# A transformer encoder-decoder layer: the two score pieces of a pair side by side, other shares of copies between VectorE and ScalarE

## The chip, the cores and the metric

The kernel runs on one core of a Trainium2 chip. TensorE multiplies matrices and transposes, VectorE and ScalarE read its results from PSUM (eight banks of 512 float32 for each of 128 partitions), GpSimd works on SBUF only, and SyncE (SP) issues the DMAs. The metric is the device time in microseconds of one execution; the figure of a kernel is the median of its runs.

## The reference

All is float32. A context of 2 x 77 rows goes through one encoder layer; 2 x 2048 rows of 512 features go through one decoder layer that attends to itself (causal) and to the context. There are 16 heads of 32.

```python
def _mha(xq, xkv, w_in, b_in, w_out, b_out, bias):
    q, k, v = ...                                   # projections, split into H heads
    scores = jnp.einsum('bhqd,bhkd->bhqk', q, k) / jnp.sqrt(hd)
    attn = jax.nn.softmax(scores + bias[None], axis=-1)
    return jnp.einsum('bhqk,bhkd->bhqd', attn, v)... @ w_out.T + b_out

x = ctx;  x = x + mha(ln(x), ln(x), bias=eb);  memory = x + ff(ln(x))
y = y + mha(ln(y), ln(y), bias=sb + causal)         # 2048 x 2048
y = y + mha(ln(y), memory, bias=cb)                 # 2048 x 77
y = y + relu(ln(y) @ ff1.T + b1) @ ff2.T + b2       # 512 -> 2048 -> 512
```

The position bias depends on the distance of query and key alone and is constant from a distance of 127 on.

## The kernel before, in words

The order of the instructions is written out by hand in Python loops; each engine works off its own queue in that order, and semaphores hold it where data or space is missing.

**Part one: causal self-attention** (to about 1,777 us), with the small encoder threaded in between. The rows of each of two batches are cut into four blocks `m` of 512 queries. For each block, each group `g` of four heads and each query tile `t` of 128 there is a *unit* (`units`). A unit in which the query tile has index `i = 4 m + t` sees `i + 1` key tiles. `pieces(i)` cuts these into pieces of at most four key tiles (512 columns); so units have one piece in a first block, two in a second, three in a third, and three or four in a fourth. Three steps work on pieces:

- `scores` (L344): four matmuls (L361), one for each head of the group, into four PSUM banks; each has 32 rows of contraction, so the four run in different row groups of the array. VectorE then evicts each bank: L370 copies the columns that need no bias into `pp` and takes the maximum with it; in the last piece of a unit, L377 does it for the 256 nearest columns with the bias added, and L384 makes the maximum of the row. For a last piece, four exps (L387, ScalarE, in place in `pp`) follow; in later blocks they are not issued at once but kept in `late_exps`, from which `exps(k)` takes k.
- `turn` (L397): the transposes of the probabilities (L411), four to a bank, and the copy of each bank to `pts` on VectorE (L415) or ScalarE (L417). A full pair of pieces has eight banks of them.
- `values` (L422): attention times V (L428), 16 matmuls for a piece of four key tiles, into a bank of its own (bank 7).

The other banks, 0 to 6, are handed out in turn by `bank()`; every step that needs a bank takes the next one, and waits until the last reader of that bank has done with it. `pp` holds the probabilities of two units, so unit `n` may be scored as far as unit `n - 2` has been turned (`may_score`, L1244).

The loop at L1262 takes the pieces of a unit in pairs. It scores what is missing, turns the pair, runs `slot(n + 1)` at the end of a unit (one projection job, L206, L217, L230 or L242, and light work such as norms, encoder stages, or the first block's cross-attention), scores one piece of a later unit, issues one or two kept exps, runs the values of the pair, and then scores further pieces if the pair had two.

**Part two: cross-attention and feed-forward of the eight blocks.** The feed-forward is done in quarter products with seven instead of eight multiplications (`PARTS`): `first_product` (L1128) has matmuls L1134, whose result is written to or accumulated in `hT` (L1145, L1147, L1149, L1151) and goes through the relu (L1154); `second_product` (L1156) has L1165 and L1173. `prepare` (L1106) forms sums of quarters (L1117) on GpSimd and VectorE three slots ahead. `ff_bank` takes banks 4 to 7 in turn. One product is done per slot; beside it, `cross(x)` (L1196) runs the next block's cross-attention by a plan of slots: norms (`norm_stages`, L718: statistics, centring L735, transposes L741, scaling and shift L745 and L747 per 128 columns), queries (`q_group`, L751), and for each of four query tiles `attend_stages` (L757): scores L768, bias and maximum L775 to L778, exp L781, division by the sum L786 to L788, transposes L794, values L805, output L814. The bias of a tile's place (`bias_tile`, L103, four DMAs) is loaded for the first two tiles of a batch's first block alone. The first block's cross-attention (`first_cross`) uses the same stages within part one.

Of the kernel before, what the change touches and what calls it, by code (L numbers as in the profile page):

```python
# [11 lines left out]
AF = mybir.ActivationFunctionType  # L12
# [5 lines left out]
P = 128  # L18
# [36 lines left out]
def tile_encoder_decoder(ctx: ExitStack, tc: tile.TileContext, ins, out):  # L55
# [93 lines left out]
    with (  # L149
# [247 lines left out]
        def turn(pieces):  # L397

            first = units[pieces[0][0]][1] == 0
            loads = []  # L400
            for n, k0, kn in pieces:
                ks = range(k0, k0 + kn)
                if first:
                    loads += [[(n, k, r) for k in ks] for r in range(HC)]
                else:
                    loads += [[(n, k, r) for r in range(HC)] for k in ks]
            for o, load in enumerate(loads):
                pt = bank()
                pts = in_turn("pts", pts_all).rearrange("p (x q) -> p x q", q=P)
                for x, (n, k, r) in enumerate(load):  # L410
                    nc.tensor.transpose(pt[:, ts(x, P)], state[n]["p"][r][:, ts(k, P)], ident)  # L411
                    got[n, k, r] = pts[:, x, :]
                w = len(load) * P
                if o % 2 if first else o >= (len(loads) + 1) // 2:
                    nc.vector.tensor_copy(pts[:, : len(load), :], pt[:, :w])  # L415
                else:
                    nc.scalar.copy(pts[:, : len(load), :], pt[:, :w])  # L417
                if o == min(3, len(loads) - 1):
                    exps(1)
            exps(1)  # L420

# [296 lines left out]
        def norm_stages(y, n, row, place, done):  # L718

            keep = {}  # L720

            def stats():
                st = sm.tile([P, 6], F32, name="bnst", tag="bnst")
                mv = sm.tile([P, 2], F32, name="cmv", tag="cmv", bufs=4)
                rs = sm.tile([P, 2], F32, name="crs", tag="crs", bufs=4)
                nc.vector.bn_stats(st, y())
                nc.vector.bn_aggr(mv, st)
                nc.vector.tensor_scalar_add(rs[:, 0:1], mv[:, 1:2], EPS)
                nc.gpsimd.tensor_tensor(rs[:, 1:2], rs[:, 0:1], mhalf[:, 0:1], ALU.pow)
                keep.update(mv=mv, rs=rs)  # L730

            def center():
                xn = keep["xn"] = place()
                mv, rs = keep["mv"], keep["rs"]
                nc.vector.tensor_scalar(xn, y(), mv[:, 0:1], rs[:, 1:2], ALU.subtract, ALU.mult)  # L735
                nc.gpsimd.tensor_tensor(y(), y(), row, ALU.add)

            def turned():
                xn, pt, dst = keep["xn"], bank(), done()
                for c in range(NC):  # L740
                    nc.tensor.transpose(pt[:, ts(c, P)], xn[:, ts(c, P)], ident)  # L741
                for c in range(NC):
                    sc, bi = vec(f"dec_{n}_s", c), vec(f"dec_{n}_b", c)
                    if c % 2:
                        nc.scalar.activation(dst[:, c, :], pt[:, ts(c, P)], AF.Identity, bias=bi, scale=sc)  # L745
                    else:
                        nc.vector.tensor_scalar(dst[:, c, :], pt[:, ts(c, P)], sc, bi, ALU.mult, ALU.add)  # L747

            return stats, center, turned

# [3 lines left out]
                nc.tensor.matmul(mm, w[:, c, :], nT[:, c, :], start=(c == 0), stop=(c == NC - 1))  # L754
            nc.vector.tensor_scalar(dst, mm, vec("dec_ca_in_b", o), SCALE, ALU.add, ALU.mult)

        def attend_stages(q, kTc, v, y, biased, pr, pts, place, w_o):  # L757

            prh = pr.rearrange("p (h k) -> p h k", k=S)
            by_r = pr.rearrange("p (g r k) -> p g r k", r=HC, k=S)  # L760
# [22 lines left out]
            def normalize():  # L783
                su = sm.tile([P, H], F32, name="csu", tag="csu", bufs=2)
                ri = sm.tile([P, H], F32, name="cri", tag="cri", bufs=2)
                nc.vector.tensor_reduce(su, prh, AX.X, ALU.add)  # L786
                nc.vector.reciprocal(ri, su)
                nc.gpsimd.tensor_tensor(prh, prh, ri[:, :, None].to_broadcast([P, H, S]), ALU.mult)  # L788

            def turned():  # L790
                for g in range(NC):
# [336 lines left out]
        def first_product(s):  # L1128
            x, layer, i, n = slots[s]
            a, b = operands[s]  # L1130
            mm = ff_bank()
            for f in range(2):
                for c in range(2):
                    nc.tensor.matmul(  # L1134
                        mm[:, ts(f, TOK)], a[:, c, ts(f, P)], b[:, c, :], start=(c == 0), stop=(c == 1)
                    )
            order = order_of(x, 1)
            got = mm.rearrange("p (f n) -> p f n", f=2)
            for k, (sign, r, c) in enumerate(PARTS[i][2]):
                users = [j for j in order if (r, c) in [u[1:] for u in PARTS[j][2]]]  # L1140
                f = (r - 1) * (NF // 2) + 2 * n
                dst = hT[:, f : f + 2, ts(c - 1, TOK)]
                if i == users[0]:
                    if sign == "-":
                        nc.scalar.activation(dst, got, AF.Identity, scale=-1.0)  # L1145
                    elif k:
                        nc.vector.tensor_copy(dst, got)  # L1147
                    else:
                        nc.scalar.copy(dst, got)  # L1149
                else:  # L1150
                    nc.vector.tensor_tensor(dst, dst, got, SIGN[sign])  # L1151
                if i == users[-1]:
                    for e in range(2):
                        nc.scalar.activation(dst[:, e, :], dst[:, e, :], AF.Relu, bias=vec("dec_ff1_b", f + e))  # L1154
# [41 lines left out]
        def cross(x):  # L1196
# [9 lines left out]
            def bias(t):  # L1206
                bias_tile(pr.rearrange("p (h k) -> p h k", k=S), 2, P, S, 255 - P * t)
# [9 lines left out]
            for t in range(TB):  # L1217
                at = 14 + 7 * t
                y = lambda t=t: y_of(x, t)
                biased = m == 0 and t < 2  # L1220
                if biased:
                    plan[at if t else at - 4].append(lambda t=t: bias(t))
                fs = attend_stages(
                    lambda g, t=t: qT[g // 2][:, g % 2, ts(t, P)], kTcs[b], vcs[b], y, biased, pr,
                    lambda g: pts_all[:S, g, :], place("xr"), wbt,
                )
                for k, f in zip((0, 2, 3, 6, 9, 11), fs):
                    plan[at + k].append(f)
                fs = norm_stages(y, "n3", bo, place("xt"), lambda t=t: nTt[:, :, ts(t, P)])
                for k, f in zip((13, 15, 17), fs):  # L1230
                    plan[at + k].append(f)
# [30 lines left out]
        while i < len(stream):  # L1262
# [17 lines left out]
            if may_score():  # L1280
                score_next()
            exps(2 if units[n][1] == 1 else 1)
            for p in pair:
                values(*p)
            while may_score() and (len(pair) > 1 or units[n][1] == 0):
                score_next()
            i += len(pair)

        xt_ring += [sb.tile([P, D], F32, name="xt", tag="xt", bufs=2) for _ in range(2)]
# [71 lines left out]
```

## Time and profile before

| | us |
|---|---|
| median of three runs (2929.42 to 2933.62) | 2931.29 |
| the profiled execution | 2935.85 |
| its span, first to last instruction | 2934.1 |
| PE busy (98%) | 2868.7 |
| DVE busy (75%) | 2205.3 |
| ACT busy (42%) | 1219.5 |
| POOL busy (25%) | 736.9 |
| mean granted TensorE clock | 0.991 |

PE is TensorE's matmuls, PEld its weight loads, DVE VectorE, ACT ScalarE, POOL GpSimd. Ends of matmuls are modelled, so a busy PE is not one at its peak; the pace is better read from the starts of one group of matmuls and the next. In a timeline line stand the start, the length, the engine, the line of the code and what is written from what, with the idle time ahead and what ended it in brackets.

### The profile page before, as it was taken

How to read it: one execution, taken by the hardware profiler on the slowest of the kernel's cores; microseconds unless marked ns; L12 is line 12 of the kernel's file. 1: busy time of each engine (PE TensorE's matmuls, PEld its weight loads, DVE VectorE, ACT ScalarE, POOL GpSimd, SP SyncE). 2: the span in 40 equal slices, each digit the busy share in tenths (PEclk: the TensorE clock that was granted, in tenths of full speed). 3: DMA queues.
4: the chain of work that ended last, by engine and by line, in shares of the span. 5: the costliest groups of instructions: out<-in, count | busy, mean ns of one | idle time of the engine just before them, and what ended most of it. 6: DMA issues, size and time to landing. Idle time of an engine off the chain costs nothing.

```text
span 2934.1 us, 60690 instructions
## 1 busy us (share of the span) xinstructions
PE 2868.7 (98%) x24440; PEld 2012.8 (69%) x24440; DVE 2205.3 (75%) x6171; ACT 1219.5 (42%) x2211; POOL 736.9 (25%) x601
## 2 busy tenths in 40 slices
PE   8899999999999999999999999999999899999999
PEld 5457666666666556666666667777777777777788
DVE  4767688878987788888888895767676767676765
ACT  3344456546665445565556672313131313131311
POOL 0100000000000101000000004555555464646465
PEclk9899999999999999999999999999999999999999
DMA  6413301201112502211101115000001000000000
GB/s 174 99 54 112 100 16 56 63 16 44 34 41 64 135 19 76 70 30 56 48 16 37 41 46 191 1 29 1 29 1 38 10 29 1 29 1 29 1 15 15
DMA packets 117644, 137.10 MB, mean 47 GB/s; under 512 B 18241, under 2 KB 73073, under 8 KB 117235
## 3 DMA queue, kind: packets, MB, share of 16 engines
q1 hardware_dynamic: 117362, 133.22, 15.7%
q8 instruction: 192, 3.15, 0.4%
q14 instruction: 90, 0.73, 0.1%
HBM read 111.33 MB, written 21.86 MB: 45 GB/s over the span
## 4 chain that ended last, share of the span: by engine, by line
PE 80%; DVE 13%; issue 2%; POOL 2%; ACT 2%; DMA 1%; SPq 0%; POOLq 0%; DVEq 0%; ACTq 0%
PE psum L1165 13%; PE psum L411 12%; PE psum L361 10%; PE psum L1134 8%; PE psum L428 7%; DVE pp L370 5%; PE psum L230 4%; PE psum L814 4%; PE psum L754 4%; PE psum L206 4%; PE psum L242 4%; PE psum L217 3%; DVE pp L377 3%; PE psum L794 2%; PE psum L805 1%
## 5 line engine op out<-in xcount | busy, mean ns | idle before, releaser
L387 ACT ACTIVATE pp<-pp,nm 128x128 f32<-128x128 f32 (+15 forms) x512 | 614.1, 1209 | 195.1 <-DVE nm L384 192.3
L370 DVE TENSOR_SCALAR_CACHE_REDUCE pp<-psum 128x512 f32<-128x512 f32 (+3 forms) x1024 | 558.0, 589 | 53.3 <-PE psum L361 51.5
L411 PE MATMUL psum<-ident,pp 128*128 128x128 f32 x4352 | 549.0, 279 | 18.0 <-DVE mx L377 11.8
L411 PEld LDWEIGHTS psum<-ident,pp 128*128 128x128 f32 x4352 | 474.5, 142 | 132.4 <-DVE pp L370 57.1
L417 ACT COPY pts<-psum 128x512 f32<-128x512 f32 (+3 forms) x592 | 298.7, 577 | 510.5 <-PE psum L411 401.3
L1117 POOL TENSOR_TENSOR vv<-pp 128x512 f32<-128x512 f32 x320 | 414.5, 1311 | 145.3 <-PE psum L1134 125.7
L361 PE MATMUL psum<-kT,q 32*128 32x512 f32 (+3 forms) x2560 | 353.5, 579 | 8.7 <-DVE mx L377 3.9
L415 DVE COPY pts<-psum 128x512 f32<-128x512 f32 (+2 forms) x544 | 329.9, 660 | 42.5 <-PE psum L411 40.8
L428 PEld LDWEIGHTS psum<-pts,vv 128*32 128x32 f32 x8704 | 226.2, 110 | 123.9 <-issue 116.9
L428 PE MATMUL psum<-pts,vv 128*32 128x128 f32 x8704 | 278.9, 276 | 0.0
L276 POOL TENSOR_TENSOR rstd<-rstd,mhalf 128x1 f32<-128x1 f32 x32 | 18.2, 570 | 919.9 <-DVE rstd L275 854.7
L1154 ACT ACTIVATE kT<-kT,vecs 128x256 f32<-128x256 f32 x256 | 115.2, 499 | 300.8 <-DVE kT L1151 300.8
L377 DVE CUSTOM_DVE_ANT_0 pp<-psum,bias 128x256 f32<-128x256 f32 (+1 forms) x512 | 209.6, 409 | 24.5 <-PE psum L361 16.6
L1151 DVE TENSOR_TENSOR kT<-kT,psum 128x512 f32<-128x512 f32 x256 | 166.4, 680 | 80.9 <-PE psum L1134 80.5
L361 PEld LDWEIGHTS psum<-kT,q 32*128 32x128 f32 x2560 | 119.6, 184 | 153.0 <-issue 99.3
L1165 PE MATMUL psum<-vv 128*128 128x256 f32 x768 | 176.9, 381 | 0.0
L1134 PE MATMUL psum<-oT,vv 128*128 128x256 f32 x736 | 166.5, 380 | 0.0
L1165 PEld LDWEIGHTS psum<-vv 128*128 128x128 f32 x768 | 143.1, 190 | 26.8 <-issue 9.5
L1134 PEld LDWEIGHTS psum<-oT,vv 128*128 128x128 f32 x736 | 138.8, 190 | 24.4 <-issue 6.2
L1117 DVE TENSOR_TENSOR vv<-kT 128x512 f32<-128x512 f32 x160 | 140.0, 892 | 10.8 <-PE psum L1165 9.8
L257 POOL TENSOR_TENSOR xr<-xr,row_dec_sa_out_b 128x512 f32<-128x512 f32 x30 | 38.1, 1274 | 375.1 <-DVE pts L415 244.3
L206 PE MATMUL psum<-nT,wqk 128*128 128x512 f32 x256 | 119.1, 609 | 0.0
(178 smaller groups left out, 3920.0 us busy)
## 6 DMA issues: line engine op xcount, KB each, us to landing
wqk<-in_dec_sa_in_wT_dram SPq DMA_DIRECT2D x64, 256.0 KB, 3.8
bias<-tz SPq DMA_DIRECT2D x128, 128.0 KB, 3.5
wbig<-in_dec_sa_in_wT_dram SPq DMA_DIRECT2D x8, 1024.0 KB, 7.3
vv<-in_enc_ff_wT_dram SPq DMA_DIRECT2D x8, 1024.0 KB, 5.4
wbig<-in_dec_sa_out_wT_dram SPq DMA_DIRECT2D x8, 1024.0 KB, 7.5
vv<-y SPq DMA_DIRECT2D x32, 256.0 KB, 3.5
out_dram<-vv SPq DMA_DIRECT2D x32, 256.0 KB, 2.0
xt<-in_x_dram SPq DMA_DIRECT2D x30, 256.0 KB, 3.9
```

Source lines behind the costliest of these rows:

```text
L206: nc.tensor.matmul(mm, w[:, c, :], nTs[b, m][:, c, :], start=(c == 0), stop=(c == NC - 1))
L361: nc.tensor.matmul(banks[r][:, : kn * P], q[rows4(r), ts(t, P)], kT[rows4(r), g, k0 * P : (k0 + kn) * P], start=True, stop=True,)
L370: nc.vector.tensor_scalar(p[:, k0 * P : (k0 + far) * P], s[:, : far * P], 1.0, None, ALU.mult, ALU.max, accum_out=st["mx"][:, r, c : c + 1],)
L377: nc.vector.tensor_tensor_reduce(p[:, (i + 1) * P - w : (i + 1) * P], s[:, far * P : kn * P], biases[b, m, g][:, r, 2 * P - w :], 1.0, LOW ...
L387: nc.scalar.activation(p, p, AF.Exp, bias=nm, accum_out=to)
L411: nc.tensor.transpose(pt[:, ts(x, P)], state[n]["p"][r][:, ts(k, P)], ident)
L415: nc.vector.tensor_copy(pts[:, : len(load), :], pt[:, :w])
L417: nc.scalar.copy(pts[:, : len(load), :], pt[:, :w])
L428: nc.tensor.matmul(ot[rows4(r), t, :], vv[:, k, ts(g * HC + r, HD)], got.pop((n, k, r)), start=(k == 0), stop=(k == i),)
L1117: engine.tensor_tensor(dst, quarter(*parts[0], n), quarter(*parts[2], n), SIGN[parts[1]])
L1134: nc.tensor.matmul(mm[:, ts(f, TOK)], a[:, c, ts(f, P)], b[:, c, :], start=(c == 0), stop=(c == 1))
L1165: nc.tensor.matmul(mm[:, t, :], lhs[:, c, ts(t, P)], rhs[:, c, :], start=(n == 0 and c == 0), stop=(n == 3 and c == 1),)
```

## The change

In part one: of the banks that a pair's turn copies, VectorE takes the first three of eight (`3 * len(loads) // 8`, rounded down; the last half before), ScalarE the others; no exp is issued amid the copies any more in later blocks; and the further pieces that may be scored are scored before the values of the pair instead of behind them, with one exp then.

In part two: all four scalings of a norm's transposes go to ScalarE (two of four were on VectorE; `first_cross` uses them too); the second of two first copies in `first_product` goes to ScalarE as well; the division of the first query tile of a block goes from GpSimd to VectorE; and the second tile's bias is loaded one slot earlier.

```diff
@@ turn
-                if o % 2 if first else o >= (len(loads) + 1) // 2:
+                if o % 2 if first else o < 3 * len(loads) // 8:
                     nc.vector.tensor_copy(pts[:, : len(load), :], pt[:, :w])
                 else:
                     nc.scalar.copy(pts[:, : len(load), :], pt[:, :w])
-                if o == min(3, len(loads) - 1):
+                if first and o == len(loads) - 1:
                     exps(1)
             exps(1)
@@ norm_stages, turned
-                    if c % 2:
-                        nc.scalar.activation(dst[:, c, :], pt[:, ts(c, P)], AF.Identity, bias=bi, scale=sc)
-                    else:
-                        nc.vector.tensor_scalar(dst[:, c, :], pt[:, ts(c, P)], sc, bi, ALU.mult, ALU.add)
+                    nc.scalar.activation(dst[:, c, :], pt[:, ts(c, P)], AF.Identity, bias=bi, scale=sc)
@@ attend_stages
-        def attend_stages(q, kTc, v, y, biased, pr, pts, place, w_o):
+        def attend_stages(q, kTc, v, y, biased, pr, pts, place, w_o, engine=None):
...
-                nc.gpsimd.tensor_tensor(prh, prh, ri[:, :, None].to_broadcast([P, H, S]), ALU.mult)
+                (engine or nc.gpsimd).tensor_tensor(prh, prh, ri[:, :, None].to_broadcast([P, H, S]), ALU.mult)
@@ first_product
-            for k, (sign, r, c) in enumerate(PARTS[i][2]):
+            for sign, r, c in PARTS[i][2]:
...
                     if sign == "-":
                         nc.scalar.activation(dst, got, AF.Identity, scale=-1.0)
-                    elif k:
-                        nc.vector.tensor_copy(dst, got)
                     else:
                         nc.scalar.copy(dst, got)
@@ cross
-                    plan[at if t else at - 4].append(lambda t=t: bias(t))
+                    plan[at - 1 if t else at - 4].append(lambda t=t: bias(t))
                 fs = attend_stages(
                     lambda g, t=t: qT[g // 2][:, g % 2, ts(t, P)], kTcs[b], vcs[b], y, biased, pr,
                     lambda g: pts_all[:S, g, :], place("xr"), wbt,
+                    None if t else nc.vector,
                 )
@@ the loop over pairs
             if may_score():
                 score_next()
             exps(2 if units[n][1] == 1 else 1)
+            while may_score() and (len(pair) > 1 or units[n][1] == 0):
+                score_next()
+            exps(1)
             for p in pair:
                 values(*p)
-            while may_score() and (len(pair) > 1 or units[n][1] == 0):
-                score_next()
             i += len(pair)
```

## The prediction

> **What bounds the kernel now.** I read the page's busy table first, then a table of stretches, then the timeline, group start against group start.
>
> ```profile
> PE 2868.7 (98%) x24440; PEld 2012.8 (69%) x24440; DVE 2205.3 (75%) x6171; ACT 1219.5 (42%) x2211; POOL 736.9 (25%) x601
> 650.00:860.00 210.00, 208.04 (x2393) 139.89 (x2393) 185.76 (x603) 128.75 (x177) 7.15 (x8) 0.98 0.12 35
> 2320.00:2934.00 614.00, 603.12 (x3497) 481.47 (x3496) 413.82 (x697) 132.25 (x259) 344.72 (x267) 1.00 0.04 15
> ```
>
> The columns of a stretch: its length, then busy PE, PEld, DVE, ACT, POOL, granted clock, DMA share, GB/s. TensorE is the bound in both parts; VectorE is at 88% in the attention of a fourth block and 67% in part two. So what counts is TensorE's stalls. Its unhindered pace is read from starts:
>
> ```profile
> 572.75 1.14 PE L361 MATMUL psum<-kT,q 32*128 32x512 f32 x8
> 573.82 1.96 PE L428 MATMUL psum<-pts,vv 128*32 128x128 f32 x64
> 575.70 1.14 PE L361 MATMUL psum<-kT,q 32*128 32x512 f32 x8
> 576.77 1.97 PE L411 MATMUL psum<-ident,pp 128*128 128x128 f32 x16
> ```
>
> Two score pieces (L361) with the values (L428) between: 1.07, 1.88, 1.07 us, no stall. Pieces of 384 and 256 columns take 0.86 and 0.645 so. A 512-column matmul has a pitch of 0.455 us (eight of L206 from 564.03 to 567.67); four heads run side by side, two matmuls each, so 0.91 of the 1.07 is work and 0.16 the step to the next kind of matmul.
>
> **Side by side: what it costs.** A piece takes four banks of a ring of seven. Two pieces with nothing between need eight: the second's fourth head writes the bank of the first's first head, and must wait until VectorE has evicted it (L370). Today the values stand in that gap. The order of the two programs' instructions gives 114 places with adjacent pieces after the change, 16 before. Those few show the price:
>
> ```profile
> 648.20 1.58 PE L361 MATMUL psum<-kT,q 32*128 32x512 f32 x14
> 649.36 0.69 DVE L370 TENSOR_SCALAR_CACHE_REDUCE pp<-psum 128x512 f32<-128x512 f32 x1 [0.32 <-PE psum L361]
> 650.11 0.29 PEld L361 LDWEIGHTS psum<-kT,q 32*128 32x128 f32 x2 [0.73 <-DVE pp L370]
> 1289.76 0.31 PEld L361 LDWEIGHTS psum<-kT,q 32*128 32x128 f32 x8 [0.20 <-issue]
> 1291.93 0.29 PEld L361 LDWEIGHTS psum<-kT,q 32*128 32x128 f32 x2 [0.50 <-DVE pp L370]
> 1292.98 0.20 PEld L411 LDWEIGHTS psum<-ident,pp 128*128 128x128 f32 x2 [0.76 <-DVE pp L370]
> ```
>
> At 648.20 VectorE was free: it starts 1.16 us after the piece (when the first scores are there) and the fourth head resumes at 1.91. With 0.91 of its own and 0.16 behind, 512 + 512 takes 2.98 us; at 1289.76, with VectorE in arrears, 3.22. Apart they take 2.14: +0.84 to +1.08. I take 0.93, nearer to the first: VectorE's three copies now come first and are done when the scores are. The other pairs likewise: 512 + 256 measured 2.70 against 1.72, unhindered 2.56: 0.9; 512 + 384 in between, 0.92; 384 + 256 measured 2.19 against 1.50: 0.69. New places: 48 x 0.93 + 22 x 0.92 + 12 x 0.9 + 10 x 0.69 = 44.6 + 20.2 + 10.8 + 6.9 = 82.5 us.
>
> With three pieces adjacent, the third waits for all four evictions of the first and one of the second. 384, 512, 512 (8 places; the first is a query tile's last piece, whose evictions take 0.74 each, below): banks free at 1.6, 2.34, 3.08, 3.82 and, one eviction (0.61, with 0.14 to the restart: 649.36, 649.97, 650.11) later, 4.65; with 0.91 + 0.16, 5.7 us against 0.86 + 3.22 today, +1.6. 512, 384, 256 (4) and 512, 512, 256 (2): four evictions from 1.16 end at 3.60, the next at 4.1 or 4.2; with 0.14 and the last head's 0.455 + 0.19 some 4.9 and 5.0 against 2.57 and 2.79, +2.3 and +2.2. The two places with five pieces (today 512, 256, 512, 512 in 8.5 us) +1.4. Together 29 us. So +112; by the rows' ends 98 to 129.
>
> **What it removes.** Transposes directly behind a tile's last piece stall today:
>
> ```profile
> 740.10 4.47 PE L411 MATMUL psum<-ident,pp 128*128 128x128 f32 x32
> 741.98 0.42 PEld L411 LDWEIGHTS psum<-ident,pp 128*128 128x128 f32 x4 [0.15 <-DVE mx L377]
> 742.73 0.42 PEld L411 LDWEIGHTS psum<-ident,pp 128*128 128x128 f32 x4 [0.33 <-DVE mx L377]
> 743.47 0.86 PEld L411 LDWEIGHTS psum<-ident,pp 128*128 128x128 f32 x8 [0.32 <-DVE mx L377]
> ```
>
> Banks come free every 0.74 us where a bank's four transposes take 0.455: 4.40 us start to start, against 3.64 without stall. All 39 such places lose 33 us. With 1.88 us of values in between, those of third and fourth blocks vanish (17 us, without the two behind the five-piece places); in second blocks the values take 0.7 to 1.0 us and the last evictions still come late, so I keep those. -17; between -10 and -33.
>
> **Copies and exps.** Of part one's 128x512 copies, 152 go from VectorE (683 ns) to ScalarE (596 ns). VectorE, not the bound, gains what TensorE cannot use. In a fourth block's tile ScalarE has ten copies and four exps of up to 2.2 us: 10 x 0.51 (four in 2.03 at 570.35) + 4 x 2.2 = 14 us, beside some 19 of TensorE (64 transposes 7.3, four pieces 4.3, values 3.8, a projection 3.6): covered. An exp now placed behind the second piece waits for its maxima with the next turn's copies queued behind it; by the same rows it ends about when the first of these can start. Taken at 0; if that fails by 0.3 us in 32 large tiles, +10.
>
> **The clock.**
>
> ```profile
> 653.00:656.50 3.50, 3.50 (x10) 1.60 (x7) 3.43 (x15) 0.00 (x0) 0.00 (x0) 0.55 0.00 0
> 656.50:660.00 3.50, 3.50 (x17) 3.32 (x17) 2.40 (x8) 1.59 (x3) 0.00 (x0) 0.50 0.00 0
> 1289.76:1292.98 3.22, 3.22 (x20) 1.36 (x17) 3.15 (x16) 0.88 (x2) 0.00 (x0) 1.00 0.00 0
> ```
>
> The granted clock (third column from the right) fell to a half for 6.8 us in the five-piece place, where banks came one by one, though no wait there was over 1.5 us; in the 3.22 us pairs it stayed at 1.00. The 14 three-piece places lie between. A fall costs about 3.4 us: 0 to 48, taken as three falls, +10. The Trainium skill ("TensorE: Matmul & The Clock Gate", part 1) has the clock halve only after an idle window of about 3.4 us; by it these places would cost nothing and the sum would be 10 lower, but the row shows a fall without such a wait.
>
> **Part two.** 92 first copies (685 ns on VectorE, 586 on ScalarE) and 128 scalings of 128x128 (about 410 and 460 ns; 112 here, 16 in part one) go to ScalarE, which is 22% busy there; seven normalisations go from GpSimd (2.25 us) to VectorE, not in the trace there: 1.4 to 1.5 us by L786 on the same 1232 elements. Behind it on VectorE stand accumulations (L1151, six in 3.61 us from 2135.79); their four banks fill at one per 1.82 us, so 1.45 us more is covered for all but a full ring.
>
> ```profile
> 2138.32 1.74 PEld L794 LDWEIGHTS psum<-ident,oT 128*77 128x77 f32 x16 [1.22 <-POOL oT L788]
> 1947.20 0.46 ACT L745 ACTIVATE vv<-psum,vecs 128x128 f32<-128x128 f32 x1 [3.15 <-DVE vv L747]
> 1947.70 0.41 DVE L747 TENSOR_SCALAR vv<-psum,vecs 128x128 f32<-128x128 f32 x1 [0.53 <-ACT vv L745]
> ```
>
> The wait for GpSimd costs TensorE 0.6 us in six blocks and more in one: -4.5. The scalings now alternate, each engine waiting for the other, and hold up VectorE's next step; TensorE loses some 1.5 us per block there, of which I take half: 7 x 1.1 = -7.5. The bias transfers (L103) moved one slot earlier on SP gain nothing: they already left at 2291.76, 0.07 us after the transposes that free their place; the stores and loads behind them on SP have several slots to spare. Sum -12; from -18 to +5, the latter if relus queue behind the added ScalarE work.
>
> **Sum.** 112 - 17 + 0 + 10 - 12 = +93 us. The profiled execution took 2935.85 us (span 2934.1 and 1.75 around it): 3029. The median of the runs, 2931.29, lies 0.16% lower: 3024.
>
> **Rivals.** *Faster, the wait is hidden:* everything but the bank wait remains. One step between kinds of matmul saved at 98 places (0.16 us each, 16 us), all 33 us of stalls gone, 18 in part two: -67, 2864 us. The Trainium skill speaks for that step ("TensorEngine Tiling (Array Packing)", key properties: a change of tiling mode drains TensorE). It decides where a wait costs under 0.3 us net per place (29 us of other savings over 98 places); every adjacent row shows 0.69 or more. 6%. *The clock falls at every pair:* 82 more places at 3.4 us, +280, about 3300 us; against it, seven 512 + 512 rows at full clock. 4%. *Nothing measurable:* waits and savings cancel, 2931; 1%. My forecast: 89%.
>
> The low end takes the waits at 98, all 33 and 18 us of savings: +47, 2975. The high end takes 129, 48 for the clock, 10 for exps, less 10 and nothing from part two: +177; I stop at 3090. About 0.2% (6 us) is what a measurement of this kernel can tell from no change. Faster 0.06, same 0.01, slower 0.93.
>
> **What would show it.** Right: L361 x16 at 2.9 to 3.2 us start to start in most tiles, its last loads waiting for DVE L370; blocks three and four longer by 0.7 to 1 us per pair; transposes behind values without stall; part two 10 us shorter. Wrong: side-by-side pieces at 2 us; clock falls in the tens; ScalarE's copies as releasers of TensorE; part two longer.

## The result, and the profile after

| | before | after |
|---|---|---|
| median, us | 2932.41 | 3020.52 |
| lowest and highest of four runs, us | 2929.42 to 2933.62 | 3012.80 to 3022.67 |
| ratio | 1 | 1.0293, 95% interval 1.0280 to 1.0306 |
| the profiled execution, us | 2935.85 | 3012.80 |
| mean granted clock in it | 0.991 | 0.990 |

The kernel became slower by 88 us. The profiled execution of after is the quickest of its four; the other three lie at 3019.86 to 3022.67 with a granted clock of 0.987 to 0.988, so sums from its trace can explain 77 us of difference (3012.80 less 2935.85).

First the busy table of the kernel after, and two of its stretches (length, then busy PE, PEld, DVE, ACT, POOL, granted clock, DMA share, GB/s).

```profile
PE 2952.2 (98%) x24440; PEld 2095.8 (70%) x24440; DVE 2032.6 (68%) x5806; ACT 1381.3 (46%) x2583; POOL 733.6 (24%) x594
650.00:860.00 210.00, 208.46 (x2244) 143.63 (x2242) 163.68 (x544) 128.04 (x185) 7.15 (x8) 0.98 0.11 32
1850.74:3010.90 1160.16, 1141.85 (x6728) 901.38 (x6724) 708.71 (x1157) 348.34 (x730) 644.04 (x497) 1.00 0.08 25
```

VectorE lost 173 us of work and ScalarE gained 162, as the change says, and TensorE is "busy" at 98% as before. The count shows what the share hides: in the same 210 us, 2244 matmuls and not 2393. The third line is part two, from the start of part one's last but one block of transposes to the end: 1160.2 us against 1168.8 before. That block itself took 5.3 us and not 4.3, in a stretch where the granted clock was 0.50 from 1850.92 to 1854.33; from its end on, part two is 9.6 us shorter.

Now a pair in the middle of a fourth block's tile, weight loads of the kernel after.

```profile
709.41 0.31 PEld L361 LDWEIGHTS psum<-kT,q 32*128 32x128 f32 x8 [0.76 <-issue]
709.94 0.63 PEld L361 LDWEIGHTS psum<-kT,q 32*128 32x128 f32 x6 [0.22 <-issue]
711.32 0.29 PEld L361 LDWEIGHTS psum<-kT,q 32*128 32x128 f32 x2 [0.75 <-DVE pp L370]
712.37 1.25 PEld L428 LDWEIGHTS psum<-pts,vv 128*32 128x32 f32 x48 [0.76 <-issue]
713.82 3.07 PEld L411 LDWEIGHTS psum<-ident,pp 128*128 128x128 f32 x28 [0.20 <-DVE mx L377]
717.26 0.42 PEld L411 LDWEIGHTS psum<-ident,pp 128*128 128x128 f32 x4 [0.37 <-DVE pts L415]
```

Sixteen score matmuls go out together; fourteen run through, the last two (the second piece's fourth head) start 1.91 us after the first, when VectorE's eviction of the bank releases them; the values start at 2.96. Behind the values 28 transposes of the next tile run without a stall; the last four wait 0.37 us for a copy of VectorE, which is new in this place. In the 2.96 us of this pair the granted clock stayed at 1.00.

TensorE's time lost, summed over part one, from the start of each group of matmuls to the start of the next, less the group's own work at 0.455 us per 512 columns (a quarter of it where four heads run side by side):

| lost in, us | before | after |
|---|---|---|
| score pieces (L361) | 92.4 | 194.1 |
| transposes (L411) behind a score piece | 33.4 | 0.7, in one place |
| transposes behind values | 19.3 | 24.7 |
| values (L428) | 17.8 | 26.1 |
| part one, with all the small groups | 167.9 | 254.3 |

A stretch at a lower clock lengthens the groups in it, so falls of the clock are inside these sums.

### The profile page after: what moved, and what is told of

Same layout as the page of the kernel before. It is cut to its first block, busy times and chain, and to the rows that moved or that the text cites. A ratio compares the mean times of both kernels' runs of the same rounds, so it can differ in the third digit from the quotient of the medians.

```text
span 3011.0 us, 60727 instructions
## 1 busy us (share of the span) xinstructions
PE 2952.2 (98%) x24440; PEld 2095.8 (70%) x24440; DVE 2032.6 (68%) x5806; ACT 1381.3 (46%) x2583; POOL 733.6 (24%) x594
## 4 chain that ended last, share of the span: by engine, by line
PE 85%; DVE 12%; ACT 1%; issue 1%; DMA 1%; SPq 0%; POOL 0%; ACTq 0%; DVEq 0%; POOLq 0%
PE psum L1160 13%; PE psum L411 12%; PE psum L361 12%; PE psum L1131 10%; PE psum L428 7%; DVE pp L370 5%; PE psum L230 4%; PE psum L811 4%; PE psum L242 4%; PE psum L206 4%; PE psum L751 4%; PE psum L217 3%; DVE pp L377 2%; PE psum L791 2%; PE psum L765 1%; PE psum L802 1%
## 5 line engine op out<-in xcount | busy, mean ns | idle before, releaser
L411 PE MATMUL psum<-ident,pp 128*128 128x128 f32 x4352 | 530.6, 277 | 7.1 <-DVE mx L377 2.9
L411 PEld LDWEIGHTS psum<-ident,pp 128*128 128x128 f32 x4352 | 475.3, 142 | 56.2 <-issue 27.9
L1114 POOL TENSOR_TENSOR vv<-pp 128x512 f32<-128x512 f32 x320 | 427.1, 1351 | 170.4 <-PE psum L1131 147.8
L361 PE MATMUL psum<-kT,q 32*128 32x512 f32 (+3 forms) x2560 | 442.8, 571 | 13.3 <-DVE pp L370 4.7
L417 ACT COPY pts<-psum 128x512 f32<-128x512 f32 (+2 forms) x744 | 373.0, 584 | 167.3 <-PE psum L411 79.0
L361 PEld LDWEIGHTS psum<-kT,q 32*128 32x128 f32 x2560 | 195.4, 185 | 238.7 <-issue 101.6
L428 PEld LDWEIGHTS psum<-pts,vv 128*32 128x32 f32 x8704 | 230.0, 111 | 115.1 <-issue 108.6
L428 PE MATMUL psum<-pts,vv 128*32 128x128 f32 x8704 | 285.4, 279 | 1.6 <-ACT pts L417 1.3
L415 DVE COPY pts<-psum 128x512 f32<-128x512 f32 (+2 forms) x392 | 237.2, 650 | 29.8 <-PE psum L411 29.6
L1146 DVE TENSOR_TENSOR kT<-kT,psum 128x512 f32<-128x512 f32 x256 | 166.7, 681 | 114.0 <-PE psum L1131 108.1
L377 DVE CUSTOM_DVE_ANT_0 pp<-psum,bias 128x256 f32<-128x256 f32 (+1 forms) x512 | 209.6, 409 | 23.6 <-PE psum L361 15.7
L1144 ACT COPY kT<-psum 128x512 f32<-128x512 f32 x124 | 69.6, 588 | 204.0 <-DVE kT L1146 135.4
```

The source lines that it names most:

```text
L361: nc.tensor.matmul(banks[r][:, : kn * P], q[rows4(r), ts(t, P)], kT[rows4(r), g, k0 * P : (k0 + kn) * P], start=True, stop=True,)
L377: nc.vector.tensor_tensor_reduce(p[:, (i + 1) * P - w : (i + 1) * P], s[:, far * P : kn * P], biases[b, m, g][:, r, 2 * P - w :], 1.0, LOW ...
L428: nc.tensor.matmul(ot[rows4(r), t, :], vv[:, k, ts(g * HC + r, HD)], got.pop((n, k, r)), start=(k == 0), stop=(k == i),)
L1114: engine.tensor_tensor(dst, quarter(*parts[0], n), quarter(*parts[2], n), SIGN[parts[1]])
```

## The experiments

Each run's ratio is to the kernel before on the same chip. They split the change first and then look for what can be kept of it.

**The order alone.**

```diff
             exps(2 if units[n][1] == 1 else 1)
+            while may_score() and (len(pair) > 1 or units[n][1] == 0):
+                score_next()
             for p in pair:
                 values(*p)
-            while may_score() and (len(pair) > 1 or units[n][1] == 0):
-                score_next()
```

> The kernel before with one edit: the further score pieces stand before the values instead of behind them; copies, exps and part two stay as before. Bank wait (my theory): the whole of part one's loss is here, since every pair of adjacent pieces waits for the eviction of the first piece's first bank: 112 us for the places, less 17 for transposes that now have values ahead of them, plus some clock falls: about 3020 to 3035 us (ratio 1.03 to 1.035); pairs of 512 + 512 at 2.96 to 3.2 us start to start. Rival 'copies': the loss comes from the bigger share of ScalarE or the later exps, then this run stays within 10 us of before.

3027.61 us, 1.0325 (1.0305 to 1.0345). The weight loads of the same pair in this kernel:

```profile
709.33 0.31 PEld L361 LDWEIGHTS psum<-kT,q 32*128 32x128 f32 x8 [0.76 <-issue]
711.25 0.29 PEld L361 LDWEIGHTS psum<-kT,q 32*128 32x128 f32 x2 [0.75 <-DVE pp L370]
712.30 0.81 PEld L428 LDWEIGHTS psum<-pts,vv 128*32 128x32 f32 x31 [0.76 <-issue]
```

The same 2.97 us, the same release. This one edit costs 94.5 us. The whole change costs 1.0293, which with part two's gain taken out (0.9971, below) is 1.0323: the order alone costs as much as all edits of part one together, and in the total the new shares of copies and exps add nothing on top of it.

The two kernels are not alike in every place, though. The granted clock of the runs with the order alone is 0.981 to 0.986, that of the kernel after 0.987 to 0.990, of the one before 0.990 to 0.993. What is missing to 1, taken of the span, is some 50, 38 and 26 us, so about 24 of the 94.5 us are falls of the clock. In the trace of the order alone, four of the eight places with pieces of 384, 512 and 512 columns end in a fall (0.50 for 3.4 or 6.8 us), and these eight take 5.96 to 6.90 us; in the kernel after they take 5.72 us, without a fall. And 15 of the 48 pairs of 512 + 512 take 3.05 to 3.23 us with the order alone, where in the kernel after 46 of them take 2.96. So the other edits of part one gain at these places and lose as much at others; where, no run takes apart.

**Is it the eighth bank?** Two kernels change only how long the wait for a bank is. In the first the ring of part one has six banks, so the second piece's third head waits too, and the fourth waits for the second eviction. In the second the first head's eviction in the middle pieces of four key tiles is halved to 256 columns (GpSimd writes zeros in the other half), so its bank comes free sooner (the other 256 scores are left out); lines behind it are numbered 3 higher.

```diff
-count = {"bank": 0, "banks": 7,
+count = {"bank": 0, "banks": 6,
```

> The changed kernel with a ring of six instead of seven banks in part one. Bank wait: the second piece's fourth head now waits for the second eviction instead of the first, one eviction (0.61 us) later: 512 + 512 at about 3.57 us instead of 2.96, some 98 pairs x 0.6 = 59 us, and more at the 14 places with three or more pieces and where transposes or a first piece meet a bank too early: 3080 to 3130 us. Rival 'step between kinds of matmul' or 'clock' (the wait is not that for a bank): 3020, pairs as before at 2.96.

```diff
                 if far:
+                    half = 2 if r == 0 and kn == 4 and not last else far
+                    if half != far:
+                        nc.gpsimd.memset(p[:, (k0 + half) * P : (k0 + far) * P], 0.0)
                     nc.vector.tensor_scalar(
-                        p[:, k0 * P : (k0 + far) * P], s[:, : far * P], 1.0, None, ALU.mult, ALU.max,
+                        p[:, k0 * P : (k0 + half) * P], s[:, : half * P], 1.0, None, ALU.mult, ALU.max,
```

> The changed kernel, but of a piece of four key tiles that is not the last of its unit the first head's eviction takes only the first 256 of 512 columns; the other 256 scores are left out (GpSimd writes zeros there, beside the work). The eviction that the second piece waits for is then 0.34 instead of 0.61 us. Bank wait: 512 + 512 at 2.70 us instead of 2.96, 82 pairs and some of the longer places x 0.27: 20 to 28 us less than the changed kernel, about 2993 to 3000 us. Rival (the second piece waits for something else, such as ScalarE's copies or the array's own queue): within 5 us of the changed kernel, pairs still at 2.96.

3126.68 us, 1.0672 (1.0647 to 1.0697), and 2999.51 us, 1.0230 (1.0215 to 1.0245). The same pair, first with six banks, then with the short eviction:

```profile
744.01 0.31 PEld L361 LDWEIGHTS psum<-kT,q 32*128 32x128 f32 x8 [0.76 <-issue]
745.92 0.29 PEld L361 LDWEIGHTS psum<-kT,q 32*128 32x128 f32 x2 [0.76 <-DVE pp L370]
746.53 0.29 PEld L361 LDWEIGHTS psum<-kT,q 32*128 32x128 f32 x2 [0.32 <-DVE pp L370]
747.58 1.25 PEld L428 LDWEIGHTS psum<-pts,vv 128*32 128x32 f32 x48 [0.76 <-issue]
```

```profile
712.51 0.31 PEld L361 LDWEIGHTS psum<-kT,q 32*128 32x128 f32 x8 [0.76 <-issue]
714.16 0.29 PEld L361 LDWEIGHTS psum<-kT,q 32*128 32x128 f32 x2 [0.48 <-DVE pp L373]
715.21 1.25 PEld L431 LDWEIGHTS psum<-pts,vv 128*32 128x32 f32 x48 [0.76 <-issue]
```

3.57, 2.96, 2.70 us: one eviction later costs 0.61, a halved one saves 0.26, and the matmuls are the same in all three. That shows the cause. The totals follow in direction: against the changed kernel's 3020.52, 106 us more and 21 us less. The first is more than 0.61 at some hundred places gives: by the sums of the table above the score pieces lose 73 us more, but also the transposes behind values 27 and the values 10, since transposes take their banks from the same ring. In both kernels the granted clock is lower as well (0.979 to 0.983 and 0.984 to 0.985, against 0.987 to 0.990); by the working above that is some 20 of the 106 us, and without it the second would have gained some 30 us and not 21. Why the clock is lower in the second, no run shows.

**Everything but the order.** The kernel after, with the values back between the score pieces (the last exp stays behind the further pieces):

```diff
             exps(2 if units[n][1] == 1 else 1)
-            while may_score() and (len(pair) > 1 or units[n][1] == 0):
-                score_next()
-            exps(1)
             for p in pair:
                 values(*p)
+            while may_score() and (len(pair) > 1 or units[n][1] == 0):
+                score_next()
+            exps(1)
```

> The changed kernel with one edit: the values stand between the two score pieces again; VectorE's three copies of eight, the later exps and all of part two stay as changed. Bank wait: with 1.88 us of values in the gap no piece waits for a bank, so part one is back at the time before and what is left is part two's gain: 2915 to 2932 us, ratio to before 0.994 to 1.000. Rival 'copies': 3000 us or more. Single 512-column pieces at 1.07 us start to start.

2986.49 us, 1.0186 (1.0171 to 1.0202). Part two gains 0.3%, so the copies and exps of part one cost about 2.2%, some 63 us, in the old order. I had priced them at nothing, and the rival's 3000 us were not reached either. Two kernels take them one at a time.

**The copies alone**, in the kernel before:

```diff
-                if o % 2 if first else o >= (len(loads) + 1) // 2:
+                if o % 2 if first else o < 3 * len(loads) // 8:
```

> The kernel before with one edit: in later blocks VectorE copies the first 3/8 of a turn's banks and ScalarE the rest, instead of ScalarE the first half. The run with the values between, 53 us slower than before, opened this question: with the transposes right behind the second score piece, VectorE is still evicting that piece when the first banks want copying, so they come free late and the next score piece waits. Theory 'first copies behind evictions': 2980 to 2995 us (most of the 53 us, plus the 9 us of part two that run had in hand); transposes ending with waits for DVE pts L415. Rival 'exps behind': the exps' new place is the cause and this run stays within 10 us of before, 2923 to 2943 us.

3008.98 us, 1.0253 (1.0238 to 1.0269). One pair's turn in its timeline, and in the last line what the weight loads of all score pieces waited for VectorE's copies (time and number; 3.3 us and 5 in the kernel before):

```profile
720.97 3.77 PE L411 MATMUL psum<-ident,pp 128*128 128x128 f32 x32
722.82 0.41 DVE L377 CUSTOM_DVE_ANT_0 pp<-psum,bias 128x256 f32<-128x256 f32 x1
722.98 0.59 ACT L417 COPY pts<-psum 128x512 f32<-128x512 f32 x1 [5.99 <-PE psum L411]
723.35 1.88 DVE L415 COPY pts<-psum 128x512 f32<-128x512 f32 x3
724.68 0.29 PEld L361 LDWEIGHTS psum<-kT,q 32*128 32x128 f32 x2 [0.18 <-DVE pts L415]
725.28 0.30 PEld L361 LDWEIGHTS psum<-kT,q 32*128 32x128 f32 x4 [0.30 <-DVE pts L415]
...
  DVE pts L415: 23.1, 89
```

The transposes start at 720.97, and their first bank is full half a microsecond later. Its copy now belongs to VectorE, and VectorE is still evicting the last score piece until 723.4 (L377 ahead of L415 in its queue). So the first three banks come free from about 724.0 on, one by one, and the score piece behind the transposes takes 2.13 us (724.68 to 726.81) and not 1.07. ScalarE, idle for 5.99 us before 722.98, had those banks in the kernel before. All waits of TensorE's weight loads for L415 over 0.1 us in part one rise from 8.4 us (15) to 56.3 (175). A load that has waited can still lie beside matmuls under way (the transposes above run to 724.74, the load behind them starts at 724.68), so such a wait is not all lost. By the sums of the table above the score pieces lose 30 us more than before, the transposes 27 and the values 4, together 61 of the 75 us. (The kept exp behind the fourth copy now stands ahead of ScalarE's last four; waits for L417 rise from 9.2 to 12.9 us only.) With the values between and all other edits of part one (the run above) the waits for L415 are the same 56.1 (175). In the kernel after they are 31.0 (104), but with the order alone and the old shares they are 28.9 (111) already: behind adjacent pieces VectorE is late with its copies whichever it has.

**The exps alone**, in the kernel before: none amid the copies in later blocks, one more at the end of each pass.

```diff
-                if o == min(3, len(loads) - 1):
+                if first and o == len(loads) - 1:
                     exps(1)
...
             while may_score() and (len(pair) > 1 or units[n][1] == 0):
                 score_next()
+            exps(1)
             i += len(pair)
```

> The kernel before with one edit: in later blocks no exp stands amid the copies of a turn, and one more stands at the end of each pass of the loop; VectorE still has the last half of the copies and the values stand between the score pieces. By my prediction (exps taken at 0): within 8 us of before, 2926 to 2942 us. Rival: a later exp makes the next turn wait for ScalarE: 2950 us or more. A third reading, that the earlier exp holds up ScalarE's copies, would give a gain of 5 us or more.

2989.15 us, 1.0186 (1.0168 to 1.0203). Its timeline at a score piece behind transposes that began at 790.01:

```profile
790.82 1.69 ACT L387 ACTIVATE pp<-pp,nm 128x1664 f32<-128x1664 f32 x1 [7.29 <-DVE nm L384]
792.50 2.03 ACT L417 COPY pts<-psum 128x512 f32<-128x512 f32 x4
793.71 0.68 PEld L361 LDWEIGHTS psum<-kT,q 32*128 32x128 f32 x4 [0.17 <-ACT pts L417]
794.59 0.30 PEld L361 LDWEIGHTS psum<-kT,q 32*128 32x128 f32 x4 [0.19 <-ACT pts L417]
```

ScalarE had been idle for 7.29 us, because the exp at the head of its queue waited for its maxima (L384). The four copies behind it, the first of whose banks was ready at about 790.5, start at 792.50. ScalarE's waits for L384 rise from 192.3 to 559.3 us, TensorE's for L417 in part one from 9.2 us (20) to 32.2 (107). By the sums of the table above the score pieces lose 34 us more, the transposes 11 and the values 4: 49 of the 54 us. So the rival of this run was right, and my price of 0 for the exps wrong in the old order. Alone the two edits cost 75 and 54 us, together (the run with the values between) 63: they do not add.

**Part two alone**, with all its edits, and the same with the second first copy left on VectorE:

> The kernel before with all edits of part two and none of part one. By the trace of the changed kernel part two is 8.6 us shorter from the start of the last transposes, whose own stall grew by 1: 2920 to 2927 us, ratio 0.996 to 0.998; TensorE's waits for L745's scalings gone, new ones for ScalarE's copies L795. Rival 'no gain': 2930 to 2936 us.

```diff
                     if sign == "-":
                         nc.scalar.activation(dst, got, AF.Identity, scale=-1.0)
+                    elif k:
+                        nc.vector.tensor_copy(dst, got)
                     else:
```

> As the run with part two alone, but the second of two first copies stays on VectorE. The waits for ScalarE's copies of the probabilities (0.71 + 0.47 us in six blocks of the changed kernel) should go if the added first copies make ScalarE late: 5 to 7 us less than part two alone, 2914 to 2921 us. Rival: they come from the scalings, or VectorE's load takes their place: no less than part two alone.

2925.92 us, 0.9971 (0.9958 to 0.9983), and 2925.78 us, 0.9968 (0.9957 to 0.9979): a gain of some 8 us, and the first copies are not part of it, for good or ill. The trace of after shows what I had missed; a block's first query tile (in kernels without L747 the lines behind it are numbered 3 lower, behind the first copies of after 5 lower: the division is L785, the transposes L791, the copies L795, the scores L765, the accumulations L1146):

```profile
2067.01 1.27 POOL L1114 TENSOR_TENSOR vv<-pp 128x512 f32<-128x512 f32 x1 [0.45 <-PE psum L1131]
2070.71 4.93 POOL L1114 TENSOR_TENSOR vv<-pp 128x512 f32<-128x512 f32 x3
2072.17 2.33 DVE L785 TENSOR_TENSOR oT<-oT,cri 128x1232 f32<-128x1232 f32 x1
2074.43 3.66 DVE L1146 TENSOR_TENSOR kT<-kT,psum 128x512 f32<-128x512 f32 x6
2074.62 1.74 PEld L791 LDWEIGHTS psum<-ident,oT 128*77 128x77 f32 x16 [1.26 <-issue]
2078.34 1.04 ACT L795 COPY pts<-psum 77x512 f32<-77x512 f32 x2
2078.96 0.30 PEld L765 LDWEIGHTS psum<-pts,bias 32*128 32x128 f32 x4 [1.04 <-ACT pts L795]
```

The division (L785) takes 2.33 us on VectorE, no less than the 2.25 on GpSimd, so the transposes (L791) wait as long as before. Six accumulations (L1146) pile up behind it; the relus that follow them stand ahead of the copies L795 in ScalarE's queue, and the next tile's scores start 0.71 us late, released by these. To see whether that reading holds, a further kernel takes the second of these two and leaves the division on GpSimd for every tile:

```diff
-                    None if t else nc.vector,
```

> Before with three of part two's edits (all four scalings on ScalarE, the bias one slot earlier, the second first copy left on VectorE), but with the division of the first query tile back on GpSimd. It tells where the two new waits of part two for ScalarE's copy of transposed probabilities (0.7 and 0.47 us in six blocks) come from. Theory: from the division on VectorE, which takes 2.34 us there while GpSimd works beside it (not 1.44) and holds up six accumulations, the relus that wait for them on ScalarE and so the copies behind those. Then those waits are gone (6 x 1.18 = 7 us less) and the wait of the transposes for GpSimd's division is back (6 x 0.6 = 3.6 us, more in the biased block: 4.5): some 2.5 us faster than with the division on VectorE, about 2923. Rival: they come from the scalings on ScalarE; then they stay and the other comes back as well, about 2930.

2919.61 us, 0.9950 (0.9936 to 0.9963).

```profile
1980.52 2.25 POOL L785 TENSOR_TENSOR oT<-oT,cri 128x1232 f32<-128x1232 f32 x1 [4.00 <-DVE cri L784]
1982.82 1.74 PEld L791 LDWEIGHTS psum<-ident,oT 128*77 128x77 f32 x16 [1.22 <-POOL oT L785]
1984.15 1.04 ACT L795 COPY pts<-psum 77x512 f32<-77x512 f32 x2
1986.45 0.98 PEld L765 LDWEIGHTS psum<-pts,bias 32*128 32x128 f32 x32 [0.33 <-issue]
```

The wait for L795 is gone in every block, the wait for GpSimd is back, and the kernel is some 5 to 6 us quicker than with the division on VectorE; the intervals of the two ratios still touch (0.9957 and 0.9963), so it is the waits in the traces that settle the reading. It is the quickest run here: 0.5% under the kernel before, 3.3% under the one after.

**Half the values between.** To save the transposes' stall without the bank wait, one piece's values go between the two score pieces and the other's behind them, where the second piece is a unit's last or another may follow (`may_score(1)` asks for the piece behind the next; its few lines are left out here):

```diff
+            rest = list(pair)
+            if len(rest) > 1 and may_score():
+                n2, k0, kn = stream[at[0]]
+                if k0 + kn == size[n2] or may_score(1):
+                    values(*rest.pop(0))
+                    score_next()
-            for p in pair:
+            for p in rest:
                 values(*p)
```

> The kernel before with the two halves of a pair's values on either side of the second score piece (score, values of the first piece, score, values of the second) where that score piece is the last of its unit or another may follow; copies, exps and part two as before. If the gap a piece needs is the 0.84 us of an eviction beyond its own length, half of the values (0.94 us and 0.16 of a step) cover it, and the other half stands ahead of the transposes, which lost 33 us at 39 places behind last pieces, and parts the adjacent pieces that lose 1.08 us at 8 places: 33 + 9, less what short values leave of it and less 0.14 us for one more step at about 80 places: 2900 to 2915 us. Rival: half of the values does not cover the eviction (VectorE in arrears), second pieces stall by some 0.3 us at 80 places, 2925 to 2950 us.

2930.81 us, 0.9993 (0.9983 to 1.0002): nothing that can be measured, where I had expected 2900 to 2915.

```profile
734.84 0.31 PEld L361 LDWEIGHTS psum<-kT,q 32*128 32x128 f32 x8 [0.76 <-issue]
738.16 2.17 PEld L411 LDWEIGHTS psum<-ident,pp 128*128 128x128 f32 x20 [0.20 <-DVE pp L370]
740.63 0.42 PEld L411 LDWEIGHTS psum<-ident,pp 128*128 128x128 f32 x4 [0.30 <-DVE mx L377]
741.37 0.86 PEld L411 LDWEIGHTS psum<-ident,pp 128*128 128x128 f32 x8 [0.33 <-DVE mx L377]
743.47 0.59 PEld L428 LDWEIGHTS psum<-pts,vv 128*32 128x32 f32 x24 [0.76 <-issue]
```

From the first piece to the values behind the next, 8.63 us; the same stretch of the kernel before, from 736.94 to 745.57, is 8.63. Moving 0.6 us of values in front of the transposes only moves the stall here: VectorE frees a bank every 0.74 us, and the last of them sets the end. By the sums of the table above the transposes lose 48 us and not 53, the score pieces 87 and not 92, and the values, now with a step more, 28 and not 18: of the 33 us that I meant to save, 5 came.

**Both**, with the second first copy on VectorE:

> The kernel before with the values split around the second score piece and part two's edits but for the first copies. If the two gains add (0.07% measured for the split, within its interval, and 0.3% for part two): 2920 to 2926 us, the same as part two alone within a measurement. Rival: they do not add, 2930 us or more.

2923.88 us, 0.9966 (0.9954 to 0.9978): part two's gain, nothing of the split.

**ScalarE five of eight, but the first five**, on top of that:

```diff
-                if o % 2 if first else o >= (len(loads) + 1) // 2:
+                if o % 2 if first else o >= len(loads) - 3 * len(loads) // 8:
```

> As the run with the split values and part two's edits less the first copies, but with the same 3/8 of the copies on VectorE as in the changed kernel at the other end of the turn: ScalarE copies the first five of eight banks, VectorE the last three. If it was the place of VectorE's copies and not their number that cost 75 us, no loss shows: within 8 us of the run with the split values and part two, so 2915 to 2932 us. Rival 'ScalarE's share': 2950 us or more, with waits for ACT pts L417.

2962.16 us, 1.0095 (1.0078 to 1.0112), 38 us more than without it.

```profile
709.58 2.06 ACT L417 COPY pts<-psum 128x512 f32<-128x512 f32 x4 [5.45 <-PE psum L411]
711.49 1.72 ACT L387 ACTIVATE pp<-pp,nm 128x1664 f32<-128x1664 f32 x1
713.17 0.61 ACT L417 COPY pts<-psum 128x512 f32<-128x512 f32 x1
713.83 0.29 PEld L361 LDWEIGHTS psum<-kT,q 32*128 32x128 f32 x2 [0.99 <-ACT pts L417]
```

The exp of 1.72 us that the kernel issues behind the fourth copy now stands ahead of the fifth, and the score piece waits 0.99 us for that bank. The weight loads' waits for L417 rise from 10.1 to 43.6 us, and the score pieces lose 38 us more. So my expectation of no loss failed, and the figure and the sign of the rival came. Whether it is ScalarE's share or only the place of the exp at the fourth of five copies stays open: no run has five first copies with the exp behind the fifth.

## Why the prediction was right, and where its steps were not

The time forecast was 3024, the measured 3020.52: the mechanism, a bank wait in place of the values, is the one that the runs with a longer and a shorter wait show, and the order alone gives as much loss as the whole change. That the forecast lies within 4 us is luck in part. The terms gave 93 us, the profiled executions differ by 77 and the medians by 88, most of the step from 77 to 88 being the lower clock of the other runs; and some terms were off in opposite directions. The terms one by one, for the profiled execution:

- **Side by side, +112.** The score pieces lost 102 us more. The price of 512 + 512 was taken at 0.93; nearly every pair measures 2.96 us, +0.82, just under the lower row (0.84). The fear that VectorE would be in arrears did not come true at these places; with the order alone it did at 15 of them, so the reason given, that VectorE's copies now come first, fits. With the measured starts (2.75 for 512 + 384, 2.54 for 512 + 256, 2.19 for 384 + 256) the pairs sum to 82 x 0.82 + 10 x 0.69 = 74 and not 82.5, and with 29 for the larger groups to 103. The three-piece estimates stood: 5.72 us against 5.7, 4.85 to 4.96 against 4.9, 4.98 against 5.0.
- **Stalls removed, -17.** Transposes lost 25.4 us and not 52.7: -27. I had kept the stalls of second blocks; most of them went too. But the values themselves lost 8 us more (17.8 to 26.1), which no step of mine had. Net -19. The transposes behind values did not run "without stall" as I had it: they lose 24.7 us where they lost 19.3, now for VectorE's copies.
- **Copies and exps, 0.** The number held, the reason did not. The sum of ScalarE's busy time (14 us beside 19) says nothing of the order in its queue, nor in VectorE's: in the old order these edits cost 75 and 54 us alone. In the new order they add nothing in the total. Part of it is that this order has brought the same kind of delay already (28.9 us of waits for VectorE's copies with the order alone, 31.0 with all), part that the score pieces lose less with them (194.1 us, 201.4 with the order alone) and the clock is higher. This is read from totals; no run takes it apart, so why the number held stays open. The queueing of copies behind an exp, which I named at 0 to +10, is real; its price is five times that in the old order. ScalarE's copies as releasers of TensorE, one of my signs of being wrong, are there in small: 9.2 us (20) before, 16.0 (46) after.
- **The clock, +10.** The mean granted clock of the profiled execution, 0.991 of 2934.1 us and 0.990 of 3011.0, means 26 and 30 us lost: +4, inside the sums of the other terms. In the other runs (0.987 to 0.988) it would be +10 to +13. The eight places of 384, 512, 512 show no fall in this execution; two of the four of 512, 384, 256 end in one of 3.4 us at 0.50 (from 403.67 and 1308.20). A fall like the one shown before came again in both five-piece places, in the first from 676.5 on:

```profile
673.00:676.50 3.50, 3.50 (x14) 1.59 (x13) 3.50 (x13) 0.00 (x0) 0.00 (x0) 1.00 0.00 0
676.50:680.00 3.50, 3.50 (x13) 2.77 (x12) 3.36 (x17) 1.88 (x2) 0.00 (x0) 0.53 0.00 0
680.00:683.50 3.50, 3.50 (x47) 2.11 (x48) 3.45 (x12) 0.00 (x0) 0.00 (x0) 0.50 0.00 0
```

  Ahead of it TensorE got one bank every 0.61 us for 4.3 us (its loads wait 0.32 each time). The rule of the Trainium skill that I weighed there ("TensorE: Matmul & The Clock Gate", part 1) has the clock halve after an idle window of about 3.4 us, so it would have no fall here; the row has one, and the measurement decides.
- **Part two, -12.** 9.6 us in the profiled execution, 8 by the run of part two alone. The step that failed is the division: taken at 1.4 to 1.5 us on VectorE from a reduction of the same elements, it takes 2.33 to 2.36 in five of seven places. So the wait of the transposes, -4.5 in my sum, stayed, and a new wait of 0.71 and 0.47 us per block came. The scalings gained more than I took: without the division's move and the first copies (which changed nothing) part two gives 15 us in place of 8, where I had 7.5 for them (the earlier bias, which I took at nothing, is in that run too and was not parted from them).

102 - 27 + 8 - 9.6 is 73; the other small groups of part one add 4: some 77 us, the difference of the two executions.

Some of the working was off without moving the forecast. The bounds 98 to 129 do not come out of the rows: 98 leaves out the ten pairs of 384 + 256, and 129 prices these too at 1.08; the rows give 105 to 125. The low end, 47 us over 2931, is 2978 and not 2975. Half of 1.5 us is not the 1.1 taken per block in part two, though it is near what TensorE's waits at these transposes come to in the trace of before (7.3 us in six blocks; none over 0.15 us after).

The rival of a hidden wait fell with its own condition: no pair under 0.69 us. The clock did not fall at every pair.

## What to carry to other kernels

Before two groups of matmuls are put side by side, count their banks: two groups of four need eight of a ring, and with seven the price is the wait for one eviction, which can be read from the few places where it happens already and tested by making the eviction longer or shorter. The busy share of an engine that is not the bound does not price a change in its queue: look at what stands ahead of the first instruction that the bound waits for. An edit that is free inside a change need not be free outside it, nor the other way round, so each part is run alone before it is kept or dropped. And where runs of one kernel differ, look at the granted clock before a difference of 10 us in 3000 is put down to an edit.

## What the hardware showed that I had not expected

An operation of VectorE with two operands in SBUF and one of GpSimd stand in each other's way. In the lines of part two above, GpSimd is in the midst of three additions when the division starts at 2072.17. The division takes 2.33 us, 0.9 more than the 1.44 us it took at 2368.96, where GpSimd did nothing; and the three additions take 4.93 us, where one takes 1.27: 1.1 us more than three. The excess is in the third addition, the one that follows the start of the division:

```profile
2073.17 2.48 POOL L1114 TENSOR_TENSOR vv<-pp 128x512 f32<-128x512 f32 x1
2364.80 3.75 POOL L1114 TENSOR_TENSOR vv<-pp 128x512 f32<-128x512 f32 x3
2368.96 1.44 DVE L785 TENSOR_TENSOR oT<-oT,cri 128x1232 f32<-128x1232 f32 x1
```

The Trainium skill ("SBUF — State Buffer", "SBUF: two separate sides") states that the two engines share one pair of ports as an exclusive lock, held for a whole instruction, also by a VectorE operation with two inputs in SBUF against a GpSimd operation that reads it. These rows agree: the division waited out the addition that was under way, and the next addition waited out the division. The rule spoke against this edit, and I had not weighed it.
